# Four-layer hybrid of attention and experts on one core: image 1's chunks of layer 1 taken half by half, with what follows an image spread over steps

## The chip, the core and the metric

The kernel runs on one core of one Trainium2 chip. The metric is the device time of one execution in microseconds (us). The engines are TensorE (PE; its weight loads, PEld, have rows of their own), VectorE (DVE), ScalarE (ACT), GpSimd (POOL) and SyncE (SP), which here only starts DMA transfers. Each engine takes its instructions in the order in which the program lists them; engines wait for each other by semaphores. L12 is line 12 of the kernel before. Matrix products write to PSUM, which has 8 banks of 128 x 512 numbers.

## What is computed

Two images of 256 channels and 32 x 32 places go through four layers; P = 128, N = 1024 places an image, CH = 512, so an image has two halves of 512 columns and eight tokens' tiles of 128. Cut to what matters here:

```python
# layer 0: group norm, attention over both images together
x = x + _L0_conv_ref(_gn(x), ...)
# layer 1: each image by itself
xn = (x - mu) * rsqrt(var + EPS) * gn_w + gn_b          # over a whole image
q, k, v = einsum('oc,bchw->bohw', w_in, xn)             # 8 heads of 64
attn = softmax(einsum('bhdi,bhdj->bhij', q * SCALE, k))
x = einsum('oc,bchw->bohw', w_out, einsum('bhij,bhdj->bhid', attn, v)) + b_out + x
# layer 2: windowed attention, then a mixture: 2 of 8 experts for each token
t = _to_tokens(x)
t = t + _L2_attn_ref(_ln_t(t), ...)
t = t + _L2_ffn_ref(_ln_t(t), ...)
# layer 3: additive attention, then a second mixture
t = t + _L3_attn_ref(_ln_t(t), ...)
t = t + _L3_ffn_ref(_ln_t(t), ...)
```

## The kernel before

**Layers 0 and 1** share one loop over steps, `attention` (L190). Its work is a list of chunks, each a pair of heads against 512 queries, and each chunk has steps over 128 keys: 64 steps in layer 0, 8 in layer 1. A step has a score (L215, L216 on PE, the exponential `e` of L218 on ACT, the running sum L227 on DVE) and an accumulation (L237 on PE). Scores run one step ahead of accumulations, two at a chunk's start. At a chunk's end ACT and DVE copy the accumulated `o` out of PSUM (L243, L244). Its tile `ps_o` exists once, so the next chunk's first accumulation waits for that copy.

Everything else hangs on steps by number: a dictionary `todo` maps a step to functions that are called after it (L268 to L292). Two steps after a chunk's end comes `divide` (L247): a row matmul L251 sums over the partitions, ACT copies the total (L257), DVE adds the two halves of o (L259), takes reciprocals (L263, two halves) and multiplies (L264), and POOL adds the reciprocals to a check (L265). Four steps after the end comes the chunk's `finish`, and four steps before the end the next chunk's `prepare`.

In layer 1 (`front`, L333) an image's norm and values are prepared amid the chunks before it (`norm` L406, `values` L429). `heads` (L438) projects q and k of one pair of heads for a whole image: two halves each, four projections into PSUM banks (L446), copied out by ACT (L450). The chunks go image by image, within it pair by pair, within that half by half (L494); so a pair's `heads` is called in front of its first half, and `finish` does its work only behind an image's last chunk. There it calls `output1` (L452): for two halves and two blocks of channels four matmuls (L457) and an addition to x on DVE (L463). Then `done` (L1427): for each of eight tiles two transposes on PE (L1432), a copy to `t` by DVE or ACT in turn, and then `norms` (L1416): statistics (L144, L145), `normalise` (L147: a square root by 13 small DVE operations, L131 to L138, a shift L153, and eight `u` by ACT, L155), and `to_channels` (L176: transposes L182 into `ps_row` banks, copied out by DVE, L186, and ACT, L184). All of these banks and those of L251, L446 and L457 come from one pool of two, taken in turn.

**Layer 0's projections** (`project0`, L509) run over four blocks of 512 columns. Ahead of blocks 0 and 2 stands the group norm of image 0 and 1 (`group_norm` L576, matmuls L542, `xn` L546), and then a block's keys, queries (L530) and values (L567).

**Behind layer 1** the window attention (L618) takes four groups of 512 tokens; POOL adds a bias to t's tiles (L647, each once its `u` is made), the groups' projections are L684, the scores L711. Then experts: a block of 128 tokens has two parts, each a step of a generator (`experts`, L1070: `turn` L1109, `up` L1126, `middle` L1137, `down` L1148), about one part for each call of `second.step()`. Image 0's blocks are done first; then `prepare` (L1526) combines its experts' results: a tile's two rows `yt` are loaded by SP and ACT queues (L1200), DVE adds them (L1202) and takes statistics; then come norm, projection (L1251) and, in the additive attention (L1266), `th` sums by DVE (L1285) and tangents by ACT (L1295). `prepare` has 12 steps: eight tiles, and two for each of two halves. Before, the experts' generator goes on in the last four of them (L1585) and then at every second group of the additive attention.

The order within these bounds is not quite that of the source: a scheduler places instructions when the program is built, so the streams of each engine are read from the built program.

Of the kernel before, what the change touches and what calls it, by code (L numbers as in the profile page):

```python
# [24 lines left out]
F32 = mybir.dt.float32  # L25
# [3 lines left out]
AF = mybir.ActivationFunctionType  # L29
ALU = mybir.AluOpType  # L30
# [57 lines left out]
class Stack:  # L88
# [101 lines left out]
    def attention(self, chunks, pools):  # L190
# [91 lines left out]

        chunks[0]["prepare"]()
        scored = 0
        for n in range(at + 5):
            ahead = 2 if 0 < n < at and steps[n][1] == 0 else 1
            while scored < min(n + ahead + 1, at):
                score(scored)
                scored += 1
            if n < at:  # L290
                accumulate(n)
            for f in todo.pop(n, []):  # L292
                f()
        nc.vector.tensor_reduce(self.extremes[:, 1:2], inverses, AX.X, ALU.max)

    def attention_pools(self, ctx):
# [36 lines left out]
    def front(self, xT, weights, tokens, done):  # L333
# [6 lines left out]
        with ExitStack() as ctx:  # L340
# [94 lines left out]
                    )  # L435
                nc.scalar.copy(v[b][:, i, :], ps)

            def heads(b, pair):  # L438

                for part, to, scale in ((0, q, 0.125), (1, k, 1.0)):  # L440
                    to[b, pair] = two.tile([P, N], F32, name="qh" if part == 0 else "kh")
                    for t in range(N // CH):
                        ps = bank()
                        for c in range(CC):
                            at = part * HID + pair * P
                            nc.tensor.matmul(  # L446
                                ps, lhsT=w_in[:, c, at : at + P], rhs=xn[b][:, c, t * CH : (t + 1) * CH],
                                start=(c == 0), stop=(c == CC - 1),
                            )
                        nc.scalar.activation(to[b, pair][:, t * CH : (t + 1) * CH], ps, AF.Copy, scale=scale)  # L450

            def output1(b):  # L452
                for t in range(N // CH):
                    for o in range(CC):
                        ps = bank()
                        for c in range(PAIRS):
                            nc.tensor.matmul(  # L457
                                ps, lhsT=w_out[:, c, o * P : (o + 1) * P],
                                rhs=oT[b][:, c, t * CH : (t + 1) * CH],
                                start=(c == 0), stop=(c == PAIRS - 1),  # L460
                            )
                        x = xT[:, o, b * N + t * CH : b * N + (t + 1) * CH]
                        nc.vector.scalar_tensor_tensor(x, ps, b_out[:, o : o + 1], x, ALU.add, ALU.add)  # L463

            def chunk1(b, pair, t):
                def prepare():
                    if t == 0 and pair:
                        heads(b, pair)

                def finish():  # L470
                    if pair == PAIRS - 1 and t == N // CH - 1:
                        output1(b)
                        done(b, bank)

                def goes_to():
                    if b not in oT:
                        oT[b] = pools1[1].tile([P, PAIRS, N], F32, name="oT")
                    return oT[b][:, pair, cols]

                cols = slice(t * CH, (t + 1) * CH)  # L480
                return {
                    "prepare": prepare,
                    "n": N // P,
                    "q": lambda: q[b, pair][:, cols],
                    "k": lambda j: [
                        k[b, pair][64 * r : 64 * r + 64, j * P : (j + 1) * P] for r in range(2)
                    ],
                    "v": lambda j: [v[b][:, j, (2 * pair + r) * 64 : (2 * pair + r + 1) * 64] for r in range(2)],
                    "o": goes_to,
                    "finish": finish,  # L490
                }

            chunks = [chunk0(t, o) for t in range(NCH) for o in range(CC)]
            chunks += [chunk1(b, p, t) for b in range(B) for p in range(PAIRS) for t in range(N // CH)]  # L494


            for b, at, first_step, apart in ((0, NCH, 8, 4), (1, NCH * CC + 5, N // P - 2, 1)):
                ready = [lambda b=b: norm(b), *(lambda b=b, i=i: values(b, i) for i in range(N // P))]
                ready += [lambda: None, lambda b=b: heads(b, 0)]
                for i, f in enumerate(ready):  # L500
                    step = first_step + apart * i
                    for c in chunks[at:]:
                        if step < c["n"]:
                            c.setdefault("extras", {}).setdefault(step, []).append(f)
                            break
                        step -= c["n"]
            self.attention(chunks, pools)

    def project0(self, pool, psum, xT, weights, to):  # L509
# [25 lines left out]

        for t in range(NCH):
            cols = slice(t * CH, (t + 1) * CH)
            if t % 2 == 0:
                b = t * CH // N
                mean, rs = self.group_norm(  # L540
                    pool, psum, xT, b,
                    lambda ps, rows: nc.tensor.matmul(ps, lhsT=group, rhs=rows, start=True, stop=True),  # L542
                )
                for at in range(b * N, (b + 1) * N, CH):
                    for c in range(CC):
                        nc.vector.tensor_scalar(  # L546
                            xn[:, c, at : at + CH], xT[:, c, at : at + CH],
                            mean[:, c : c + 1], rs[:, c : c + 1], ALU.subtract, ALU.mult,
                        )


            for o in range(CC):
                ps = project(wk, o, t)
                for r in range(2):
                    mine, other = (slice(64 * a, 64 * a + 64) for a in (r, 1 - r))
                    to = k[mine, 2 * o + r, cols]
                    if r:
                        nc.scalar.activation(to, ps[mine], AF.Identity, bias=bk[mine, o : o + 1])
                    else:
                        nc.vector.tensor_scalar(to, ps[mine], bk[mine, o : o + 1], None, ALU.add)  # L560
                    nc.sync.dma_start(out=k[other, 2 * o + r, cols], in_=to)
# [820 lines left out]
    def run(self):  # L1382
        tc, nc, ins = self.tc, self.nc, self.ins
        PER = N // P
        with ExitStack() as ctx:
            window = ExitStack()
            xw = window.enter_context(tc.tile_pool(name="wa_in", bufs=1, side="right"))
            with tc.tile_pool(name="xT", bufs=1, side="right") as xp:
# [19 lines left out]
                def norm(which, g, bank):  # L1408

                    tiles = slice(4 * g, 4 * g + 4)  # L1410
                    t, u, uT, mv = (have[n] for n in ("t", "u", "uT", "mv"))
                    rs = self.normalise(u[:, tiles], t[:, tiles], mv[:, which, tiles], 1e-5)
                    self.to_channels(uT[:, :, g * CH : (g + 1) * CH], u[:, tiles], bank)
                    return mv[:, which, tiles, 1], rs

                def norms(which, b, bank):  # L1416

# [6 lines left out]
                        self.to_channels(uT[:, :, g * CH : (g + 1) * CH], u[:, 4 * g : 4 * g + 4], bank)  # L1424
                    return mv[:, which, tiles, 1], rs

                def done(b, bank):  # L1427

                    for i in range(b * PER, (b + 1) * PER):
                        ps = bank(0)[:, 0:C].rearrange("p (c d) -> p c d", c=CC)  # L1430
                        for c in range(CC):
                            nc.tensor.transpose(ps[:, c, :], xT[:, c, i * P : (i + 1) * P], self.ident)  # L1432
                        to = have["t"][:, i, :].rearrange("p (c d) -> p c d", c=CC)
                        if i % 2:
                            nc.scalar.copy(to, ps)
                        else:
                            nc.vector.tensor_copy(to, ps)
                    norms(0, b, bank)

                self.front(xT, weights, tokens, done)  # L1440
                t, u, uT = (have[n] for n in ("t", "u", "uT"))
# [123 lines left out]
            with ExitStack() as side:  # L1565
# [16 lines left out]
                        inv.close()  # L1582
                    second.step()
                for k, _ in enumerate(prepare(0, bank, enter(side, "outputs2"), PER, nc.sync, nc.scalar)):
                    if k >= PER:  # L1585
                        second.step()


# [43 lines left out]
class General(Stack):  # L1632
# [4 lines left out]
    def front(self, xT, weights, tokens, done):  # L1637
# [2 lines left out]
        self.layer1(xT, *weights())  # L1640
        tokens()
        with self.tc.tile_pool(name="tok_ps", bufs=4, space=PSUM) as psum:
            for b in range(B):
                done(b, lambda k: psum.tile([P, CH], F32, name="tr"))

    def attention(self, chunks, pools):

# [540 lines left out]
```

## Time and profile before

| | |
|---|---|
| time, median of 3 runs | 2505.05 us (2500.96 to 2509.13) |
| profiled execution: its own time | 2506.88 us |
| its span, first to last instruction | 2504.9 us |
| PE, DVE, ACT busy | 94%, 68%, 57% of the span |
| mean clock granted to PE | 0.978 |
| layer 0's first score, layer 1's last row matmul | at 63.5 and 1352.5 us |
| first scores of the window attention | at 1386.1 us |
| image 0's first `yt` starts, first tangent | at 1713.3 and 1746.7 us |

A row of a timeline has the start, the duration, the engine, the line, the operation, what it writes and reads, how many instructions are put together, and in brackets how long the engine had been idle and what released it. A row of waits has who waited, for whom, the total in us, how often, and the longest. A row of busy times by stretch has the length, then the busy us of PE, PEld, DVE, ACT and POOL with their instructions, the clock granted to PE (1 is full), the DMA's share and GB/s.

### The profile page before, as it was taken

The page shows a single profiled execution, that of the slowest core. Times are in us where ns is not written, and L with a number is a line of the kernel's source. Part 1 is how long each engine was busy: PE and PEld are TensorE (multiplying, and loading weights), DVE is VectorE, ACT ScalarE, POOL GpSimd, SP SyncE. Part 2 cuts the span into 40 slices and gives each one's busy share as a digit, 9 for nine tenths or more (in the row PEclk, how much of TensorE's full clock was granted, in tenths as well). Part 3 has the DMA queues.
Part 4 walks back from the last instruction along what each step waited for, and adds up shares of the span by engine and source line. Part 5 has one row for each costly group of instructions (what it writes and reads, how often), then busy time and mean ns, then how long its engine had stood idle before and what let it go on. Part 6 is the DMA issues. An engine that isn't in the chain of part 4 may idle for free.

```text
span 2504.9 us, 42385 instructions
## 1 busy us (share of the span) xinstructions
PE 2350.2 (94%) x17211; PEld 1024.5 (41%) x17211; DVE 1701.1 (68%) x2616; ACT 1436.9 (57%) x1626; POOL 241.6 (10%) x254
## 2 busy tenths in 40 slices
PE   7999999999999999999999969997999988889997
PEld 4333333333333333333333536664444432334664
DVE  5677777775677777876578566326877788886543
ACT  1565556545555566544454333222999999999222
POOL 0000000000000000000001312221110000111342
PEclk9999999999999999999999989998999999999998
DMA  4000000000000000000000036775343202122896
GB/s 139 1 1 1 1 1 1 1 1 1 1 1 1 1 2 1 1 1 1 1 2 9 3 117 244 297 289 208 137 141 136 90 14 78 66 91 93 305 323 236
DMA packets 58928, 190.50 MB, mean 76 GB/s; under 512 B 14116, under 2 KB 28964, under 8 KB 48740
## 3 DMA queue, kind: packets, MB, share of 16 engines
q1 hardware_dynamic: 45236, 161.86, 18.3%
q0 software_dynamic: 8160, 22.29, 2.5%
q10 hardware_dynamic: 5328, 3.55, 0.5%
q8 instruction: 137, 2.24, 0.4%
q14 instruction: 67, 0.55, 0.1%
HBM read 168.15 MB, written 17.43 MB: 74 GB/s over the span
## 4 chain that ended last, share of the span: by engine, by line
PE 70%; DVE 11%; issue 7%; ACT 6%; DMA 3%; POOL 1%; SPq 0%; ACTq 0%; DVEq 0%; POOLq 0%
PE ps_o L237 20%; PE ps_t L215 19%; PE ps_e L1304 7%; PE bk_h L1130 4%; PE bk_y L1154 4%; ACT th L1295 3%; DVE sum L227 2%; PE ps_row L446 2%; PE ps_pt L1325 2%; DVE th L1285 2%; PE ps_qk L530 1%; PE ps_row L432 1%; DVE den L263 1%; DMA w<-in_l_w 1%; PE ps_row L457 1%
## 5 line engine op out<-in xcount | busy, mean ns | idle before, releaser
L227 DVE TENSOR_TENSOR sum<-sum,e 128x1024 f32<-128x1024 f32 x592 | 724.9, 1224 | 303.5 <-ACT e L218 292.6
L218 ACT ACTIVATE e<-ps_t 128x1024 f32<-128x1024 f32 x640 | 653.4, 1025 | 464.9 <-PE ps_t L216 463.4
L237 PE MATMUL ps_o<-e,v 64*64 64x512 f32 x5120 | 677.0, 592 | 8.5 <-DVE o L244 7.9
L215 PE MATMUL ps_t<-q,k 64*64 64x512 f32 x2048 | 533.0, 591 | 0.5 <-DVE v L571 0.5
L216 PE MATMUL ps_t<-q,k 64*64 64x512 f32 x2048 | 533.0, 591 | 0.0
L1285 DVE TENSOR_SCALAR th<-kT,qb 128x1024 f32<-128x1024 f32 x478 | 331.2, 749 | 90.2 <-PE ps_e L1304 87.9
L237 PEld LDWEIGHTS ps_o<-e,v 64*64 64x64 f32 x5120 | 194.1, 132 | 370.8 <-issue 179.4
L1295 ACT ACTIVATE th<-th 128x4096 f32<-128x4096 f32 x94 | 335.8, 3651 | 5.2 <-DVE th L1285 5.2
L1146 ACT ACTIVATE h<-bk_t,w 128x128 f32<-128x128 f32 x496 | 142.5, 375 | 267.2 <-issue 149.8
L1304 PE MATMUL ps_e<-th,pick 128*32 128x512 f32 x2048 | 270.2, 621 | 25.4 <-ACT p L1357 15.0
L215 PEld LDWEIGHTS ps_t<-q,k 64*64 64x64 f32 x2048 | 149.2, 133 | 287.2 <-issue 152.9
L1130 PE MATMUL bk_h<-w,xgT 128*128 128x512 f32 x496 | 242.9, 606 | 10.3 <-DVE xgT L1118 9.9
L1154 PE MATMUL bk_y<-w,h 128*128 128x256 f32 x992 | 247.9, 385 | 3.0 <-issue 1.0
L1154 PEld LDWEIGHTS bk_y<-w,h 128*128 128x128 f32 x992 | 178.3, 192 | 48.7 <-issue 24.0
L1135 DVE COPY hp<-bk_h 128x512 f32<-128x512 f32 x124 | 85.3, 688 | 121.6 <-PE bk_h L1130 121.5
L265 POOL TENSOR_TENSOR inverses<-inverses,den 128x512 f32<-128x512 f32 x24 | 30.5, 1269 | 1325.0 <-DVE den L263 1325.0
L216 PEld LDWEIGHTS ps_t<-q,k 64*64 64x64 f32 x2048 | 149.3, 133 | 0.0
L215 PE MATMUL ps_t<-qh,kh 64*64 64x512 f32 x512 | 139.4, 602 | 0.0
L216 PE MATMUL ps_t<-qh,kh 64*64 64x512 f32 x512 | 138.5, 600 | 0.0
L1304 PEld LDWEIGHTS ps_e<-th,pick 128*32 128x32 f32 x2048 | 58.3, 112 | 172.0 <-issue 115.2
L1161 POOL DMA_INDIRECT given<-y,gives x85 | 87.0, 1023 | 428.8 <-DVE y L1160 358.4
L1130 PEld LDWEIGHTS bk_h<-w,xgT 128*128 128x128 f32 x496 | 86.9, 193 | 80.8 <-issue 54.8
(335 smaller groups left out, 2053.6 us busy)
## 6 DMA issues: line engine op xcount, KB each, us to landing
w<-in_l_w SPq DMA_DIRECT2D x39, 1152.0 KB, 5.4
w<-in_l_w SPq DMA_DIRECT2D x39, 1030.0 KB, 7.0
w<-in_l_w SPq DMA_DIRECT2D x46, 640.0 KB, 6.7
w<-in_l_w SPq DMA_DIRECT2D x46, 514.0 KB, 5.4
rows<-u SPq DMA_DIRECT2D x8, 512.0 KB, 3.7
yt<-given SPq DMA_DIRECT2D x24, 128.0 KB, 2.3
k<-k SPq DMA_DIRECT2D x16, 128.0 KB, 2.2
uT<-given ACTq DMA_DIRECT2D x16, 128.0 KB, 4.1
```

The lines of the kernel that those rows point to most:

```text
L215: nc.tensor.matmul(ps[part, 0, :], lhsT=ka[:, part], rhs=q[0:64, :], start=True, stop=True)
L216: nc.tensor.matmul(ps[part, 1, :], lhsT=kb[:, part], rhs=q[64:128, :], start=True, stop=True)
L218: nc.scalar.activation(e, ps, AF.Exp)
L227: nc.vector.tensor_tensor(c["sum"], c["sum"], e, ALU.add)
L237: nc.tensor.matmul(c["po"][64 * r : 64 * r + 64, half, :], lhsT=v[part, :], rhs=e[part, r, :], start=(j == 0), stop=(j == c["n"] - 1),)
L1130: nc.tensor.matmul(ps, lhsT=inputs[b][:, c, :], rhs=first[b][:, at : at + CH], start=(c == 0), stop=(c == CC - 1),)
L1146: nc.scalar.activation(hidden[b, n][:, cols], ps[:, cols], AF.Gelu, bias=first[b][:, at : at + 1])
L1154: nc.tensor.matmul(sums[b], lhsT=h[:, j * P : (j + 1) * P], rhs=second[b][:, at : at + C], start=(n == 0 and j == 0), stop=(n == HH - 1 an ...
L1161: nc.gpsimd.indirect_dma_start(out=given[b], out_offset=index(slots(b)[1], b), in_=y, in_offset=None)
L1285: nc.vector.tensor_scalar(h[:, j, :], *keys_and_queries(n, j), None, ALU.add)
L1295: nc.scalar.activation(h, h, AF.Tanh)
L1304: nc.tensor.matmul(scored[i][U * j : U * (j + 1), a, :], lhsT=aa["pick"][:, m, :], rhs=h[:, j, a * CH : (a + 1) * CH], start=(m == 0), sto ...
```

## The change

Four edits; what is computed stays the same.

1. Image 1's chunks go half by half: all four pairs of its first half, then all four of the second. `heads` now projects k (both halves) with a pair's first half, and q of one half at a time. Image 0 keeps its order. The keys of pairs 2 and 3 of image 1 are put into the place of image 0's values, since they are now held over both halves.
2. What follows an image is a list of small functions, one for each of the next steps: for each half two outputs, four tiles (`token`, now with its statistics) and one norm over four tiles. Image 0's fourteen come after its last chunk, image 1's seven of the first half after its chunk of pair 3, first half, and seven of the second half at the end.
3. In `project0` the group norm of image 1 stands ahead of block 1 instead of block 2.
4. In image 0's combination one more `second.step()` is called, after the third tile.

```diff
-        for n in range(at + 5):
+        n = 0
+        while n < at or todo:
...
             for f in todo.pop(n, []):
-                f()
+                for i, g in enumerate(f() or []):
+                    later(n + 1 + i, g)
+            n += 1
...
-            def heads(b, pair):
-                for part, to, scale in ((0, q, 0.125), (1, k, 1.0)):
-                    to[b, pair] = two.tile([P, N], F32, name="qh" if part == 0 else "kh")
-                    for t in range(N // CH):
...
+            def heads(b, pair, t):
+                for i in (t,) if b else range(0 if t else N // CH):
+                    q[b, pair, i] = two.tile([P, CH], F32, name="qh", bufs=4)
+                    project(b, pair, 0, i, q[b, pair, i])
+                if t:
+                    return
+                if b and pair >= 2:
+                    if not spare:
+                        spare.append(pools1[0].tile([P, N // P, HID], F32, name="v"))
+                    at = (pair - 2) * (N // CH)
+                    k[b, pair] = spare[0][:, at : at + N // CH, :].rearrange("p a d -> p (a d)")
+                else:
+                    k[b, pair] = two.tile([P, N], F32, name="kh")
+                for i in range(N // CH):
+                    project(b, pair, 1, i, k[b, pair][:, i * CH : (i + 1) * CH])
...
                 def prepare():
-                    if t == 0 and pair:
-                        heads(b, pair)
+                    if pair or t:
+                        heads(b, pair, t)
 
                 def finish():
-                    if pair == PAIRS - 1 and t == N // CH - 1:
-                        output1(b)
-                        done(b, bank)
+                    if pair == PAIRS - 1 and (b or t):
+                        follow = []
+                        for i in (t,) if b else (0, 1):
+                            follow += [lambda i=i, o=o: output1(b, i, o) for o in range(CC)]
+                            follow += done(b * (N // CH) + i, bank)
+                        return follow
...
-            chunks += [chunk1(b, p, t) for b in range(B) for p in range(PAIRS) for t in range(N // CH)]
+            chunks += [chunk1(0, p, t) for p in range(PAIRS) for t in range(N // CH)]
+            chunks += [chunk1(1, p, t) for t in range(N // CH) for p in range(PAIRS)]
...
-            if t % 2 == 0:
-                b = t * CH // N
+            if t < B:
+                b = t
...
-                    rs = self.normalise(u[:, tiles], t[:, tiles], mv[:, which, tiles], 1e-5)
+                    self.normalise(u[:, tiles], t[:, tiles], mv[:, which, tiles], 1e-5, scalar=which == 0)
...
-                def done(b, bank):
-                    for i in range(b * PER, (b + 1) * PER):
...
-                    norms(0, b, bank)
+                def token(i, bank):
...
+                    stats(0, i)
+                def done(g, bank):
+                    return [*(lambda i=i: token(i, bank) for i in range(4 * g, 4 * g + 4)), lambda: norm(0, g, bank)]
...
-                    if k >= PER:
+                    if k == 2 or k >= PER:
                         second.step()
```

In the built programs PE has 17214 rows of instructions before and after, ACT, POOL and SP keep their numbers too, and DVE has more, since a square root's 14 small operations are now made for four tiles at a time and not for eight.

More of the change, by code (lines that the diff above doesn't have):

```diff
@@ L436, in values @@
                 nc.scalar.copy(v[b][:, i, :], ps)
-            def heads(b, pair):
-                for part, to, scale in ((0, q, 0.125), (1, k, 1.0)):
-                    to[b, pair] = two.tile([P, N], F32, name="qh" if part == 0 else "kh")
-                    for t in range(N // CH):
[L443 to L463, printed above, removed]
+            def project(b, pair, part, t, to):
+                ps = bank()
+                for c in range(CC):
+                    at = part * HID + pair * P
+                    nc.tensor.matmul(
+                        ps, lhsT=w_in[:, c, at : at + P], rhs=xn[b][:, c, t * CH : (t + 1) * CH],
+                        start=(c == 0), stop=(c == CC - 1),
+                    )
+                nc.scalar.activation(to, ps, AF.Copy, scale=1.0 if part else 0.125)
@@ new lines, in front @@
+            spare = []
+            def heads(b, pair, t):
[13 more added lines that the diff above has]
+                    project(b, pair, 1, i, k[b, pair][:, i * CH : (i + 1) * CH])
@@ new lines, in output1 @@
+            def output1(b, t, o):
+                ps = bank()
+                for c in range(PAIRS):
+                    nc.tensor.matmul(
+                        ps, lhsT=w_out[:, c, o * P : (o + 1) * P], rhs=oT[b][:, c, t * CH : (t + 1) * CH],
+                        start=(c == 0), stop=(c == PAIRS - 1),
+                    )
+                x = xT[:, o, b * N + t * CH : b * N + (t + 1) * CH]
+                nc.vector.scalar_tensor_tensor(x, ps, b_out[:, o : o + 1], x, ALU.add, ALU.add)
@@ L483, in chunk1 @@
                     "n": N // P,
-                    "q": lambda: q[b, pair][:, cols],
+                    "q": lambda: q[b, pair, t],
                     "k": lambda j: [
@@ L493, in front @@
             chunks = [chunk0(t, o) for t in range(NCH) for o in range(CC)]
-            chunks += [chunk1(b, p, t) for b in range(B) for p in range(PAIRS) for t in range(N // CH)]
+            chunks += [chunk1(0, p, t) for p in range(PAIRS) for t in range(N // CH)]
+            chunks += [chunk1(1, p, t) for t in range(N // CH) for p in range(PAIRS)]
             for b, at, first_step, apart in ((0, NCH, 8, 4), (1, NCH * CC + 5, N // P - 2, 1)):
                 ready = [lambda b=b: norm(b), *(lambda b=b, i=i: values(b, i) for i in range(N // P))]
-                ready += [lambda: None, lambda b=b: heads(b, 0)]
+                ready += [lambda: None, lambda b=b: heads(b, 0, 0)]
                 for i, f in enumerate(ready):
@@ L1411, in norm @@
                     t, u, uT, mv = (have[n] for n in ("t", "u", "uT", "mv"))
-                    rs = self.normalise(u[:, tiles], t[:, tiles], mv[:, which, tiles], 1e-5)
+                    self.normalise(u[:, tiles], t[:, tiles], mv[:, which, tiles], 1e-5, scalar=which == 0)
                     self.to_channels(uT[:, :, g * CH : (g + 1) * CH], u[:, tiles], bank)
-                    return mv[:, which, tiles, 1], rs
                 def norms(which, b, bank):
@@ L1425, in norms @@
                     return mv[:, which, tiles, 1], rs
-                def done(b, bank):
-                    for i in range(b * PER, (b + 1) * PER):
[L1430 to L1437, printed above, removed]
-                    norms(0, b, bank)
+                def token(i, bank):
+                    ps = bank(0)[:, 0:C].rearrange("p (c d) -> p c d", c=CC)
+                    for c in range(CC):
+                        nc.tensor.transpose(ps[:, c, :], xT[:, c, i * P : (i + 1) * P], self.ident)
+                    to = have["t"][:, i, :].rearrange("p (c d) -> p c d", c=CC)
+                    if i % 2:
+                        nc.scalar.copy(to, ps)
+                    else:
+                        nc.vector.tensor_copy(to, ps)
+                    stats(0, i)
+                def done(g, bank):
+                    return [*(lambda i=i: token(i, bank) for i in range(4 * g, 4 * g + 4)), lambda: norm(0, g, bank)]
                 self.front(xT, weights, tokens, done)
@@ L1642, in front @@
         with self.tc.tile_pool(name="tok_ps", bufs=4, space=PSUM) as psum:
-            for b in range(B):
-                done(b, lambda k: psum.tile([P, CH], F32, name="tr"))
+            for g in range(NCH):
+                for f in done(g, lambda k: psum.tile([P, CH], F32, name="tr")):
+                    f()
     def attention(self, chunks, pools):
```

## The prediction

> **What bounds the kernel now.** I read the page's busy times and the chain that ended last first, then TensorE's (PE's) own list of waits, then the timelines around the places that the diff touches.
>
> ```profile
> PE 2350.2 (94%) x17211; PEld 1024.5 (41%) x17211; DVE 1701.1 (68%) x2616; ACT 1436.9 (57%) x1626; POOL 241.6 (10%) x254
> ...
> PE 70%; DVE 11%; issue 7%; ACT 6%; DMA 3%; POOL 1%; SPq 0%; ACTq 0%; DVEq 0%; POOLq 0%
> ```
>
> PE is busy for 94% of the span and carries 70% of the chain. PE's instructions are the same in both built programs (17214 in each); only their order differs. So the change can move the time by nothing but PE's waits and by the clock that PE gets. All waits of PE for a release that the changed places own are in these rows (line, what it waited for: total us, times, longest us):
>
> ```profile
> PE bk_t L1141 <- ACT h L1146: 9.9, 3, 7.2
> ...
> PE ps_o L237 <- DVE o L244: 7.9, 7, 1.2
> PE ps_gs L542 <- DVE gn_mv L586: 7.5, 1, 7.5
> PE ps_qk L530 <- DVE xn L546: 6.6, 2, 3.4
> ...
> PE ps_row L182 <- ACT u L155: 5.9, 5, 3.0
> ```
>
> The reader is to see how small they are: everything that spreading image 0's and image 1's follow-up can win is L182's 5.9 us and part of L237's 7.9, plus what the clock loses after a wait. That loss shows at image 0's norm:
>
> ```profile
> 1207.77 0.59 PE L237 MATMUL ps_o<-e,v 64*64 64x512 f32 x1
> 1210.73 0.33 PE L182 MATMUL ps_row<-ident,u 128*128 128x128 f32 x1 [2.38 <-ACT u L155]
> ```
>
> ```profile
> 1210.00:1219.00 9.00, 8.11 (x23) 2.71 (x23) 1.63 (x4) 6.13 (x11) 0.00 (x0) 0.62 0.01 2
> ```
>
> PE stands 2.4 us, and then (busy times of that stretch, the clock behind POOL's column) gets a clock of 0.62 for 9 us, which is 3.4 us of work lost. The price of that wait is 2.5 + 3.4 = 5.9 us.
>
> What VectorE (DVE) does in one chunk of image 1 decides the rest:
>
> ```profile
> 1247.34 1.23 DVE L227 TENSOR_TENSOR sum<-sum,e 128x1024 f32<-128x1024 f32 x1 [0.79 <-ACT e L218]
> 1248.92 3.36 DVE L263 RECIPROCAL den<-total 128x256 f32<-128x256 f32 x2 [0.36 <-ACT total L257]
> 1252.21 1.77 DVE L264 TENSOR_TENSOR oT<-o,den 128x256 f32<-128x256 f32 x2
> 1253.90 5.20 DVE L227 TENSOR_TENSOR sum<-sum,e 128x1024 f32<-128x1024 f32 x4
> 1259.02 0.69 DVE L244 COPY o<-ps_o 128x512 f32<-128x512 f32 x1
> ```
>
> Each chunk's divide holds DVE for 3.36 + 1.77 = 5.1 us; then it catches up at 1.23 us for a sum against PE's 1.72 us a step (starts of neighbouring score steps, 1303.32 and 1305.04). It runs late for half a chunk, and whatever stands behind the reciprocals in its queue is late with it.
>
> **The follow-up, spread (image 0 both halves, image 1's first half).** Before, an image's eight tokens were normed after the last divide had long gone by. Now there are three sets of two outputs, four tokens and a norm, each amid the next chunks. I followed each set along the built program's queues, with R for the start of the divide's row matmul L251. DVE starts the reciprocals at R + 1.9 (1224.88 to 1226.79). Norm chain: 13 small operations at 0.2 us (1206.37 to 1210.05, one sum of 1.2 taken off) and a shift; statistics 0.36; the first u 0.5 and 0.15 to reach PE.
>
> Set 1 (image 0, tokens 0 to 3): DVE's queue holds reciprocals, last token's statistics, sum, 7 small operations, sum, 6 more, shift: 1.9 + 3.4 + 0.4 + 1.2 + 0.1 + 1.4 + 1.2 + 1.2 + 0.2 + 0.65 = R + 11.65. PE comes to the norm's transposes after the row (1.0), the last token (0.43), two steps (3.44) and a quarter of a third (1.07): R + 5.95. **Wait 5.7 us.** Behind it on PE stand the rest of that accumulation, the next scores, three projections and two outputs; ScalarE (ACT) has the four u's ahead of the next exponential, and DVE waits for that exponential, so nobody else gets ahead.
>
> Set 2 (image 0, tokens 4 to 7): the chain stands ahead of the reciprocals. From the last token's transposes PE has one step, the row and half a score: 3.15. DVE needs 0.1 + 0.4 + two statistics 0.9 + 2.4 + sum 1.2 + 0.4 + 0.65 = 6.1. **Wait 3.0.** Then the first transposed bank is emptied only behind reciprocals and products (5.1), and the next projection wants that bank: PE is there at about 11.0, the bank free at 12.9. **Wait 1.9.**
>
> Set 3 (image 1, first half): reciprocals and products both ahead, with two sums and the chain behind: 1.9 + 3.4 + 1.8 + 0.4 + 1.2 + 0.7 + 1.2 + 2.0 + 0.2 + 0.65 = R + 13.4; PE is there at R + 6.2. **Wait 7.2.**
>
> Together 17.8. After each, the clock and the pacing by ACT's u's (0.5 us each): the nearest rows are 3.4 (above) and 1.5 (0.96 over 38 us from 1352, where a wait of 3.0 lies). I take 2.8 a set, 8.4. Sum **+26.2**; bounds: +13 (half the waits, 1.5 each) and +34 (POOL's add of L265, 1.26 us, also holds each set's sum up; 3.4 for each clock, and 2 more for waits as long as these).
>
> [...]
>
> **What goes.** Image 0's wait above: -5.9. L237's waits for o in image 1: three of 1.2 us (the rows of that stretch say 3.6, 3 times), each at the end of a chunk that has no projections in it; now every chunk but the last has 1.7 us of projection (7.13 us for four, L446), which is more than 1.2: -3.6 (bounds 0 and -3.6).
>
> **The end of image 1.** Before, from the last row matmul PE lost 1.3 at tokens, 3.3 for u and 1.6 by the clock. Now half of the outputs and tokens are gone from there (PE does them earlier, at the same price), and with them cover. The last two outputs' first three products (5.1) end 0.9 before oT (6.0 after the row; a bias product, L641, fills half). Then tokens and eight projections of the window stage hold PE for 9, while DVE needs 12: POOL's adds L647 now start ahead of the chain, and beside those adds small DVE operations took 0.65 to 0.71 instead of 0.17 (1374.02 to 1379.5). 0.5 + 3.0 + 1.6 + 1.0 against 6.2: I take 0, bounds -4.7 (chain not held up) and +3.
>
> **First group norm.** Moved from ahead of t = 2 to ahead of t = 1. Before:
>
> ```profile
> 36.75 0.35 PE L542 MATMUL ps_gs<-gs_d,group 128*128 128x2 f32 x2 [1.15 <-DVE gs_d L606]
> 40.48 5.28 PE L530 MATMUL ps_qk<-xn,sb_wk 128*128 128x512 f32 x8 [3.37 <-DVE xn L546]
> ```
>
> 1.15 + 3.37 and 1.7 by the clock (5.28 for what takes 3.6 elsewhere): 6.2. Now xn is long ready at t = 2, but PE's first average stands behind statistics that DVE starts only behind t = 0's v: 25.55 + 3.0 = 28.5 against PE's 25.2, so 3.4, then 1.1, then the same 1.7: 6.2. Net **0**, bounds -1.7 and +1.7. Image 1's data were there at 25.55 without a wait, and SP's k copies keep their place.
>
> **The experts' part amid image 0's combination.**
>
> ```profile
> 1711.92 1.89 PE L1154 MATMUL bk_y<-w,h 128*128 128x256 f32 x8
> 1721.03 1.12 PE L1141 MATMUL bk_t<-ident,hp 128*128 128x128 f32 x4 [7.22 <-ACT h L1146]
> 1726.77 2.08 PE L1130 MATMUL bk_h<-w,xgT 128*128 128x512 f32 x2 [4.62 <-DVE xgT L1118]
> ```
>
> PE has 11.8 us idle here, and a part is 4.2 us of PE (8.33 us a block, two parts). But the end of the stage is set by DVE: combinations, norm, u at 1729.4, keys, first tangent at 1746.7. The part puts y, hp and three half xgT into that queue ahead of u (0.4 + 0.7 + 1.1), and the last xgT waits for PE to have finished the part: u at about 1733.8, **+4.4**. ACT takes four gelus between its DMA issues, so the last yt goes out at 1720.2 instead of 1720.05. SP's fetches and POOL's scatter of the part come that much earlier and are waited for by nobody there. In the stage after it, where ACT is busy 49.9 of 50 us and PE 48.8, the part's 4.2 us of PE (or only ACT's 1.1) are gone: -2.4. Net **+2**, bounds -4 and +4.4.
>
> **Sum** against the profiled execution (2506.9; span 2504.9 and 2.0 around it): 26.2 - 5.9 - 3.6 + 0 + 0 + 2 = +18.7, so 2525.6. The median of the three runs, 2505.05, is 1.8 lower: **2524**. A measurement of this kernel tells about 0.3%, 7.5 us, from no change.
>
> **Rivals.**
> Faster: the norm's chain is done when PE comes to the transposes at L182. A set then costs nothing there, and what goes wins: -5.9 - 3.6 and about -2 at the ends: 2505 - 11 = 2494. The sign turns where the three sets cost 11.5 together, 3.8 each. For: set 2's chain stands ahead of the reciprocals, and a PE that is 5 us later than I count would meet it everywhere. Against: the reciprocals' 3.36 us lie in each of 24 chunks, and nothing in sets 1 and 3 lets the chain pass them. 0.13.
> Nothing to be seen: the sets cost some 13, the lower bound: 2505 + 13 - 9.5 = 2508. For: the waits may overlap with a clock that is low anyway. 0.17.
> Much slower: the clock stays half through the transposes that ACT's u's pace, as after the 7.2 and 4.6 above (0.80 over 35 us from 1710, 7 us lost); then each set costs 4 more: 2537. 0.15.
> My forecast, 2512 to 2532: 0.55. So faster 0.13, same 0.17, slower 0.70. The range leaves out most of the faster case and takes in the others: 2500 to 2538.
>
> **What would show it.** Right: between 1200 and 1330 three waits of L182 for u of about 6, 3 and 7 us, each with a clock below 1 behind it; a projection L446 that waits for uT's copy; in image 1 no wait for o but perhaps one; u of the combination some 4 us later with a shorter wait for h; the start of the first scores as before, near 63.5. Wrong: L182's waits in sum as before, or layer 1 ending earlier than at 1386 (the window scores' start, now expected near 1402).

## The result, and the profile after

The change makes the kernel slower: 2532.41 us in the median of four runs (2529.9 to 2535.3) against 2505.89 in four runs of before taken beside them, a ratio of 1.0107 (95% interval 1.0093 to 1.0121). The profiled execution took 2535.32 us with a span of 2533.0, so it is some 3 us longer than the median.

Lines of the kernel after are shifted: L446, L450 and every line up to L284 have the same numbers as before; L475 are the output products (L457 before), L1451 the tokens' transposes (L1432), L564 and L552 the first group norm and its projections (L542, L530), L706 and L762 the window's projections and averages (L684, L740), L1163 and L1152 the experts' (L1141, L1130). The page of after, busy times and the chain by engine:

```profile
PE 2370.5 (94%) x17211; PEld 1030.1 (41%) x17211; DVE 1705.3 (67%) x2644; ACT 1435.6 (57%) x1626; POOL 241.9 (10%) x254
...
PE 71%; DVE 11%; issue 7%; ACT 6%; DMA 3%; POOL 1%; SPq 0%; ACTq 0%; DVEq 0%; POOLq 0%
```

PE has the same 17211 matmul records and 20.3 us more busy time: much of the loss is not idle time but work at a lower clock, which takes 51.2 us of PE's busy time in after and 35.5 in before (busy time times what the granted clock was below 1; its mean is 0.971 for 0.978). PE's waits over the whole kernel after, in the rows that the prediction showed of before:

```profile
PE ps_row L182 <- ACT u L155: 18.3, 4, 6.1
...
PE ps_gs L564 <- DVE gn_mv L608: 11.0, 2, 7.5
...
PE bk_t L1163 <- ACT h L1168: 5.3, 3, 2.8
...
PE ps_o L237 <- DVE o L244: 4.2, 4, 1.2
...
PE ps_qk L552 <- DVE xn L568: 3.3, 1, 3.3
```

L182 went from 5.9 to 18.3 us, L237's waits for o from 7.9 to 4.2. The waits of the group norm only changed rows (7.5 + 6.6 before, 11.0 + 3.3 after). PE's timeline shows L182's four waits, those of the sets 1, 2 and 3 and of the last set, at the end of image 1:

```profile
1221.02 1.39 PE L182 MATMUL ps_row<-ident,u 128*128 128x128 f32 x4 [5.46 <-ACT u L155]
...
1255.94 0.33 PE L182 MATMUL ps_row<-ident,u 128*128 128x128 f32 x1 [2.27 <-ACT u L155]
...
1335.37 0.69 PE L182 MATMUL ps_row<-ident,u 128*128 128x128 f32 x2 [6.11 <-ACT u L155]
...
1402.88 0.69 PE L182 MATMUL ps_row<-ident,u 128*128 128x128 f32 x2 [4.41 <-ACT u L155]
```

What holds set 1 up stands in DVE's timeline:

```profile
1210.73 3.37 DVE L263 RECIPROCAL den<-total 128x256 f32<-128x256 f32 x2 [0.35 <-ACT total L257]
1214.02 0.37 DVE L144 BATCH_NORM_STATS2 ln_st<-t 128x6 f32<-128x256 f32 x1
1214.30 2.29 DVE L227 TENSOR_TENSOR sum<-sum,e 128x1024 f32<-128x1024 f32 x1
...
1217.87 1.22 DVE L227 TENSOR_TENSOR sum<-sum,e 128x1024 f32<-128x1024 f32 x1
...
1220.17 0.16 DVE L153 SCALAR_TENSOR_TENSOR nm_shift<-mv,rs 128x4 f32<-128x4 f32 x1
```

The reciprocals stand ahead of the last statistics, the sums between them and the small operations, and the shift ends 11.5 us after the start of the row matmul (1208.82); PE had come to the transposes at 1215.56.

Where the time is, stage by stage in the profiled executions (lengths in us; each stage ends at the event named, the last at the end of PE's last instruction and the others at a start):

| stage, until | before | after | e3 | e9 | e12 |
|---|---|---|---|---|---|
| first score | 63.5 | 65.0 | 65.5 | 65.1 | 64.7 |
| window's first average (L740, L762) | 1327.0 | 1346.6 | 1346.9 | 1322.8 | 1324.4 |
| first expert's transpose | 104.7 | 105.7 | 106.5 | 103.9 | 104.4 |
| image 0's first `yt` start | 218.1 | 222.5 | 217.5 | 215.3 | 216.8 |
| first tangent | 33.5 | 36.2 | 34.5 | 34.8 | 36.2 |
| last tangent | 558.2 | 557.9 | 560.6 | 558.3 | 556.8 |
| PE's last instruction | 191.5 | 190.5 | 191.4 | 190.9 | 188.7 |

19.6 of the 28 us lie in the second row, and there in layer 1 and what follows it: layer 0, from its first score to layer 1's, takes 929.7 us for 929.6. The 4.4 us in the experts' blocks and the 1.5 at the start cannot be told from scatter: over all 14 profiles of this study the blocks took 212.2 to 222.5 us and the first score came at 62.9 to 65.8, whichever edits a kernel had.

### The profile page after: what moved, and what is told of

The parts are those of the page before. It is cut to its first block, busy times and chain, and to the rows that moved or that the text cites. A ratio compares the mean times of both kernels' runs of the same rounds, so it can differ in the third digit from the quotient of the medians.

```text
span 2533.0 us, 42411 instructions
## 1 busy us (share of the span) xinstructions
PE 2370.5 (94%) x17211; PEld 1030.1 (41%) x17211; DVE 1705.3 (67%) x2644; ACT 1435.6 (57%) x1626; POOL 241.9 (10%) x254
## 4 chain that ended last, share of the span: by engine, by line
PE 71%; DVE 11%; issue 7%; ACT 6%; DMA 3%; POOL 1%; SPq 0%; ACTq 0%; DVEq 0%; POOLq 0%
PE ps_o L237 20%; PE ps_t L215 20%; PE ps_e L1326 6%; PE bk_y L1176 4%; PE bk_h L1152 4%; ACT th L1317 3%; PE ps_row L446 2%; DVE sum L227 2%; DVE th L1307 2%; PE ps_pt L1347 2%; PE ps_qk L552 1%; PE ps_row L436 1%; PE ps_row L475 1%; PE bk_t L1163 1%; DVE den L263 1%
## 5 line engine op out<-in xcount | busy, mean ns | idle before, releaser
L237 PE MATMUL ps_o<-e,v 64*64 64x512 f32 x5120 | 679.2, 592 | 4.9 <-DVE o L244 4.2
L237 PEld LDWEIGHTS ps_o<-e,v 64*64 64x64 f32 x5120 | 194.1, 132 | 365.2 <-issue 180.0
L1152 PE MATMUL bk_h<-w,xgT 128*128 128x512 f32 x496 | 244.4, 608 | 10.8 <-DVE xgT L1140 10.0
L1152 PEld LDWEIGHTS bk_h<-w,xgT 128*128 128x128 f32 x496 | 87.5, 193 | 78.1 <-issue 54.2
L1123 POOL DMA_INDIRECT xg<-rows,takes x85 | 89.3, 1050 | 276.3 <-PE bk_x L1135 223.3
L215 PE MATMUL ps_t<-qh,kh 64*64 64x512 f32 x384 | 105.0, 603 | 0.0
```

The source lines that it names most:

```text
L215: nc.tensor.matmul(ps[part, 0, :], lhsT=ka[:, part], rhs=q[0:64, :], start=True, stop=True)
L237: nc.tensor.matmul(c["po"][64 * r : 64 * r + 64, half, :], lhsT=v[part, :], rhs=e[part, r, :], start=(j == 0), stop=(j == c["n"] - 1),)
L1123: nc.gpsimd.indirect_dma_start(out=tokens[b], out_offset=None, in_=rows(b)[:, :], in_offset=index(slots(b)[0], b))
L1152: nc.tensor.matmul(ps, lhsT=inputs[b][:, c, :], rhs=first[b][:, at : at + CH], start=(c == 0), stop=(c == CC - 1),)
```

## The experiments

My theory: readers of a norm's result stand in in-order queues for a chain that DVE finishes some 5 us too late, and the clock adds to it. Rivals: the other edits; the order half by half in itself; follow-up work strewn among steps in itself; DVE as the bound. Each time stands beside runs of before on the same chip (medians 2508.92 for e1 to e4, 2505.23 for e5 to e8, 2508.51 for e9 to e11, 2506.11 for e12). The ratios are the recorded ones and not the quotients of these medians; the quotient is 1.0076 for e3, 1.0051 for e4, 1.0090 for e8 and 1.0122 for e10, and within 0.0006 of the ratio elsewhere.

| | kernel | time, us | ratio (95% interval) |
|---|---|---|---|
| e1 | before + first group norm moved | 2509.03 | 0.9998 (0.9985 to 1.0012) |
| e2 | before + experts' part | 2508.91 | 1.0000 (0.9984 to 1.0016) |
| e3 | follow-up and order alone | 2527.89 | 1.0056 (1.0037 to 1.0076) |
| e4 | e3 with image 1 in the old order | 2521.72 | 1.0043 (1.0029 to 1.0057) |
| e5 | e3, u and transposes later | 2513.47 | 1.0036 (1.0019 to 1.0054) |
| e6 | e3, transposes alone later | 2516.20 | one run |
| e7 | e3, whole norm later | 2513.34 | one run |
| e8 | e3, waits filled with matmuls | 2527.77 | 1.0079 (1.0063 to 1.0096) |
| e9 | e3, u on POOL, transposes later | 2503.48 | 0.9981 (0.9964 to 0.9998) |
| e10 | e8 with half the filling | 2539.07 | 1.0136 (1.0110 to 1.0162) |
| e11 | order alone, follow-up in bursts | 2518.52 | 1.0045 (1.0031 to 1.0058) |
| e12 | the whole change, u on POOL | 2506.29 | 1.0004 (0.9990 to 1.0018) |

**e1 and e2: the two small edits.** In before:

```diff
-            if t % 2 == 0:
-                b = t * CH // N
+            if t < B:
+                b = t
```

> The kernel before with only the first group norm of image 1 moved from ahead of t = 2 to ahead of t = 1. My theory: its waits change place and not size (3.4 + 1.1 us at the averages ahead of t = 1 for 1.15 + 3.37 us at t = 2, and 1.7 us by the clock on both sides), so the first score starts within 1.5 us of the 63.48 us of before and the time within 2 us of 2505.9. Rival: the first queries and keys of t = 1 stay at a low clock behind the new wait, and the 1.5 us by which the first score of the changed kernel is late (65.02) are all this edit's; then 2507.4. Either way it is no part of the 27 us that matters.

First score at 63.3 us; e3, without this edit, has it at 65.5. So the edit is worth nothing that these runs can show, and the 1.5 us of the changed kernel are not its.

```diff
-                    if k >= PER:
+                    if k == 2 or k >= PER:
                         second.step()
```

> The kernel before with only the experts' part amid image 0's combination. My theory: first tanh about 3 to 4 us later against the first yt copy than before, some 2 us of it won back in the additive stage; total +1.5 to +2, 2507 to 2508, and the blocks between 1495 and 1713 as long as before (218.1 us). Rival: the 4.4 us by which the blocks of the changed kernel took longer (222.5 for 218.1) come from this edit, by the fetches that it moves on SP's queue; then the blocks are 222 us long here too, and the time is about 2512.

The blocks took 216.6 us, and the time is not the 2512 of the rival that blamed SP's queue, so that rival falls. From the first `yt` to the first tangent it took 36.8 us instead of 33.5, and nothing of that came back (558.2 us of tangents before, 561.5 here).

**e3 and e4: follow-up and order.** e3 is the change without those two edits. e4 is e3 with

```diff
-            chunks += [chunk1(1, p, t) for t in range(N // CH) for p in range(PAIRS)]
+            chunks += [chunk1(1, p, t) for p in range(PAIRS) for t in range(N // CH)]
...
-                    if pair == PAIRS - 1 and (b or t):
+                    if pair == PAIRS - 1 and t:
...
-                        for i in (t,) if b else (0, 1):
+                        for i in (0, 1):
```

> The changed kernel without the moved group norm and without the experts' part amid the combination: image 1 half by half and the spread follow-up alone. My theory: nearly all of the loss is here. Three waits at L182 for u of 5.5, 2.3 and 6.1 us, a clock near 0.5 to 0.6 behind each, a wait of 4.4 us at the last norm; +18 to +23 up to the window stage's end, 2524 to 2530. Rival: the loss is shared by the late stages, and this kernel stands at 2518 or below.

> As the kernel with the follow-up alone, but image 1 in the old order (pair by pair, both halves) with its whole follow-up behind the last chunk: only image 0's follow-up is spread. My theory: two sets are left (waits 5.5 and 2.3 us, 4.4 and 1.4 us by the clock, 13.5 in all), image 0's old wait goes (-5.9) and the waits for o in image 1 go by the projections that now stand ahead of each chunk (-2 to -3.6): +4 to +6, 2510 to 2512. Rival: the half-by-half order itself costs nothing but its third set, or the spread alone costs the whole loss: then 2520 or above. Second rival: spreading image 0's follow-up wins and only the order loses: below 2505.

e3 has the waits of the changed kernel to 0.02 us (5.47, 2.27, 6.12, 4.41), and layer 1 takes 1346.9 us. e4 was meant to lose 4 to 6 us and lost 11 by its ratio (7 to 14): its two sets wait as foreseen (5.47 and 2.27), but a third cost that I had not seen joins them at the end of image 1. There the follow-up goes half by half now, and on PE the second half's outputs stand behind the first half's norm. The waits from 1180 to 1410:

```profile
PE ps_row L182 <- ACT u L155: 13.2, 3, 5.5
PE ps_row L251 <- DVE sum L227: 2.7, 1, 2.7
PE ps_mm L706 <- ACT qh L711: 1.1, 1, 1.1
PE ps_row L1451 <- DVE xT L480: 0.7, 1, 0.7
```

13.2 less 5.47 and 2.27 leaves 5.4 us at the first half's norm, for the 3.0 of before.

**e5, e6, e7: readers later.** In e5 a set's functions, one to a step and in shorthand, are

```diff
-  [*tokens, norm]
+  [*tokens, chain, nothing, nothing, nothing, scaled, nothing, turned]
```

with `chain` DVE's square root and shift, `scaled` ACT's four u, `turned` PE's transposes. e6 calls `scaled` with `chain`, e7 the whole norm after the three empty steps.

> The kernel with the follow-up alone, but of each norm only DVE's chain (1/sqrt and shift) stays in its step; ACT's four u come four steps later and PE's transposes of them two steps after those. DVE's queue is the same. My theory (who reads the chain's result comes 5 us too early): the waits at L182 of 5.5, 2.3 and 6.1 us go, and the low clock behind them (6.7 to 8.3 us in all three) with them; against the follow-up alone -20 to -22, so 2506 to 2509 beside 2508.9 for before; the wait at the last norm (4.4 us) stays. First rival (what costs is that follow-up work is strewn among the steps: switches between small transposes and scores, PE's banks, ACT's extra work): the waits go but the time falls by less than half of that, to 2518 or more. Second rival: the waits return in another row (scores for exponentials, projections for banks), and the time hardly falls.

> As above, but ACT's four u stay with the chain and only PE's transposes come four steps later. My theory: ACT then stands in its queue for the chain (some 5 us for sets 1 and 3, 2 for set 2) with the next exponentials behind it, so L182 waits no more but PE stands at L237 for e, or at L215 for a score bank, for what is left after PE's lead of one to two steps (1.7 to 3.4 us): 2 to 4 us each for sets 1 and 3. Span between the two. Rival: only PE's own place matters, ACT has slack for it (busy 57%): then no wait is left and the span is that of the kernel where both come later.

> The follow-up alone, but each norm as a whole (chain, u and transposes) three steps later, so that the divide's reciprocals are done with when DVE comes to the chain. My theory: sets 1 and 3 lose what the reciprocals hold the chain up by and keep the chain's own length, as set 2 has it now: three waits of 2 to 3.5 us in place of 5.5, 2.3 and 6.1, each with a low clock behind it; 6 to 9 us of the wait and clock go. Rival (the chain itself with its sums between is what takes the time, not the reciprocals): waits of 5 us or more stay.

I had expected e5 to come out as before; it stands 8 us above. In none of the three does L182 wait amid the steps any more, and in each, waits of 4 to 5.5 us stand elsewhere. e5's waits of PE from 1180 to 1420, ACT's timeline and PE's around set 1:

```profile
PE ps_o L237 <- ACT e L218: 7.8, 3, 5.1
PE ps_row L182 <- ACT u L1472: 4.4, 1, 4.4
PE ps_row L446 <- ACT qh L450: 4.0, 1, 4.0
```

```profile
1211.56 1.02 ACT L218 ACTIVATE e<-ps_t 128x1024 f32<-128x1024 f32 x1 [0.75 <-PE ps_t L216]
1218.82 0.60 ACT L1472 ACTIVATE u<-t,nm_shift,rs 128x256 f32<-128x256 f32 x1 [6.23 <-DVE nm_shift L1468]
1219.32 0.58 ACT L450 ACTIVATE qh<-ps_row 128x512 f32<-128x512 f32 x1
```

```profile
1214.47 1.45 PE L446 MATMUL ps_row<-xn,sb_l_w_in 128*128 128x512 f32 x3
1219.95 2.08 PE L446 MATMUL ps_row<-xn,sb_l_w_in 128*128 128x512 f32 x2 [4.03 <-ACT qh L450]
```

ACT stands 6.23 us at the first u with the copy of a projection behind it, and PE then waits for that copy. The shift ends 11.53 us after the row matmul in all three kernels (sets 1; 12.2 in sets 3), as in the changed one. The edits did not do to ACT and DVE what I had written: in sets 1 and 3 the scheduler put chain and u where they had been, u two exponentials behind the last token's copy, and only PE's transposes moved. So e7 says nothing of reciprocals and chain apart, and the three runs are one experiment: freeing PE alone takes away about half, since ACT still stands in line. From layer 1's first score to the window's first average e3 is 19.8 us longer than before; in e5 8.7 of these are left, in e6 12.3 and in e7 10.5.

**e8 and e10: is it the clock?** Ahead of the transposes:

```diff
+                    if which == 0:
+                        ps = bank(0)
+                        for _ in range((12, 5, 14, 10)[g]):
+                            nc.tensor.matmul(ps, lhsT=self.ident, rhs=xT[:, 0, 0:CH], start=True, stop=True)
```

> The follow-up alone, with 12, 5, 14 and 10 matmuls of 128x512 (0.43 us each) that nobody reads ahead of the transposes of the four norms; PE works through its waits. The output is the reference's. It takes nothing from the waits: u comes when it came. What it tells is the price of the clock: by the profile 3 to 4.4, 1.7 to 3.3, 2 and 4 us behind the four waits. My theory: L182's waits shrink to under 1 us each, the granted clock stays 1.0 through the sets, and the time falls by 11 to 14 against the follow-up alone, to 2514 to 2517. Rival: the clock behind a wait costs nothing, since the transposes are paced by ACT's u there anyway; then the time stays at 2526 to 2530.

> The kernel with filled waits again, with half the filling (6, 2, 7 and 5 matmuls; one was meant as 0.43 us and takes 0.87, so the first filling lasted 35.8 us for 18.3 us of waits). Now 5.2, 1.7, 6.1 and 4.4 us. My theory: PE works through its waits and no longer; the clock stays 1.0 behind all four; 12 us of low clock go and no more than 1 to 2 us are added: -10 to -12 against the follow-up alone, 1.002 to 1.004 of before against its 1.0056 to 1.0079. Rival: a low clock behind the waits costs little, since the u pace the transposes: 1.006 or more again.

A matmul of that shape stands in the records as two of 0.43 us, so e8's filling lasted 35.8 us for 18.3 us of waits. The clock did stay 1.0 behind all four, and from image 1's values to the first window average what PE lost by the low clock fell against e3 from 14.1 to 1.7 us and its idle time from 24.3 to 7.2; but the filling cost as much as that gave. e10 (6, 2, 7, 5) was to be clean and is the slowest of all: the scheduler put the filling two steps earlier than the wait began, so that those steps came behind it, and the exponentials they feed as well.

```profile
1212.22 5.42 PE L1438 MATMUL ps_row<-xT,ident 128*128 128x512 f32 x12
1220.16 1.39 PE L182 MATMUL ps_row<-ident,u 128*128 128x128 f32 x4 [2.53 <-ACT u L155]
```

Both runs fail as a price of the clock; that comes from the traces (last section).

**e11: the order alone.** As e3, but `finish` calls outputs, tokens and norm at once, image 0's eight tokens with one chain.

> Image 1 half by half (with the projections spread over its chunks), but every follow-up at once where its last divide is, as before: image 0's after its last chunk, image 1's first half amid the second half's first chunk, the second half's at the end. My theory: image 0's old wait stays (2.4 us and 3.4 by the clock), the two halves of image 1 have a burst each with a wait of 3 to 5 us and 2 to 4 by the clock, and the waits for o go (-3.6): +3 to +8, 1.001 to 1.003 of before; so most of the 19 to 27 us come from spreading and not from the order. Rival: the order itself is the loss, 1.005 or more.

+10 us by the medians and +11 by the ratio, above the range I gave. Image 0's wait is the old one (2.40, and 0.77 for a bank), the first half's burst waits 3.14 and the last norm 4.40 instead of 3.00; 10.2 us are lost by the low clock there, 5.0 before. So order and spread each cost by themselves: in the table's second row 9.2 us (e11) and 13.3 (e4), and 19.9 together (e3).

**e9: nobody waits for the chain but POOL.** As e6, where `scaled` comes with `chain`, with

```diff
+                            if g < 3:
+                                nc.gpsimd.tensor_scalar(
+                                    u[:, 4 * g + i, :], t[:, 4 * g + i, :],
+                                    mv[:, 0, 4 * g + i, 0:1], got["rs"][:, i : i + 1], ALU.subtract, ALU.mult
+                                )
+                                continue
```

in `scaled`, and `turned` seven steps behind `chain` instead of four.

> The follow-up alone, with the twelve u of the three sets amid the steps computed by POOL instead of ACT, and PE's transposes of them seven steps later; the last set's u stay on ACT. Two runs with later readers left waits of 4 to 5 us where PE waits for a projection's copy or an exponential: in both programs ACT's u stand behind the same two exponentials as without the delay, so ACT waits for DVE's chain there and all its later work waits with it. My theory (who stands in a queue for the chain costs, be it PE or ACT): with nobody but POOL waiting, the waits at L446 and L237 for ACT (11.6 us in the run where u and transposes came later) and the low clock behind the first and third (4 us) go; beside that run -12 to -15, so 2498 to 2502 in that job's terms, 0.996 to 0.999 of before. Rival: DVE itself is the bound there (reciprocals, products, sums and chain, late by itself by 5 us); then the exponentials wait for DVE's sums (four e buffers), waits of 2 to 5 us stay, and the time is 1.002 of before or more.

This is the run that decides. All of PE's waits of 0.3 us or more from 1180 to 1400, and POOL's u of set 1:

```profile
PE ps_row L182 <- ACT u L1478: 4.3, 1, 4.3
PE ps_row L251 <- DVE sum L227: 2.7, 1, 2.7
PE ps_o L237 <- DVE o L244: 1.7, 2, 1.4
PE ps_o L237 <- ACT e L218: 0.3, 1, 0.3
```

```profile
1220.46 6.18 POOL L1473 TENSOR_SCALAR u<-t,mv,rs 128x256 f32<-128x256 f32 x4 [4.90 <-DVE nm_shift L1468]
```

DVE is as late as ever (the shift ends 11.51 us after the row matmul), POOL takes 6.18 us for what took ACT 2.08, and PE waits for none of it: the waits of the three sets are gone and none like them has come in their place. So DVE is not the bound, and strewing work among the steps costs little by itself. e9 differs from e6 in two things, the engine that makes u and three more steps for the transposes. What was left of e6's waits stood behind ACT, so it is the first that answers them; the two were not run apart. The table's second row is 24.1 us shorter than in e3 and 4.2 shorter than before, and the kernel is the only one to beat before, by 0.2%, with an interval that ends just under 1.

**e12: the whole change so.** The same `done` in the changed kernel.

> The changed kernel whole, with the moved group norm and the experts' part, and with the twelve u of the three sets on POOL and their transposes seven steps later. My theory: the loss of the change is the wait of ACT and PE for the norms' chain and the clock behind it, and the other two edits are worth nothing to 2 us: 0.997 to 1.000 of before, and no wait for u but the last one (4.3 us). Rival: group norm and experts' part cost something together with the spread follow-up (the changed kernel measured 1.0107 [1.0093, 1.0121], the follow-up alone 1.0056 [1.0037, 1.0076], each of the two others alone 1.000): then it stands 3 to 5 thousandths above the 0.998 of the follow-up with POOL's u, at 1.001 to 1.003.

From 1180 to 1400 the same waits as in e9, and 1.0004, between my range (to 1.000) and the rival's (from 1.001): the change is repaired down to before, not below it. Whether the two small edits cost something in company stays open: alone they are 1.000 each, but after stands at 1.0107 for e3's 1.0056 (1.0076 by the medians), and e12 at 1.0004 for e9's 0.9981, the last two with overlapping intervals.

## Why the prediction was right, and where not

The direction and the mechanism were right; the time came 8 us above my 2524, at the upper edge of the forecast (2512 to 2532) and within the range. That it came so near is in part luck: the sets cost 4.3 us less than my sum and the end of image 1 4.3 more, and the two errors cancel. By its steps:

- **Three sets**, +26.2 in my sum. Waits 5.46, 2.27 and 6.11 for my 5.7, 3.0 and 7.2; the 1.9 us at a bank that waits for uT did not appear (no such row). The clock behind them took 4.4, 1.7 and 1.9 us (busy time times what the clock was below 1) for my 8.4. In all 21.9. That it comes from queues that stand for DVE's late chain is shown by e9 and e12; that the reciprocals in particular do is read from DVE's rows and was not tested, since e7 did not move the chain.
- **What goes**, -5.9 and -3.6: right. L237's waits fell by 3.7, and the old burst is gone.
- **The end of image 1, "I take 0"**: this term failed. It had the bounds -4.7 and +3 and measured +4.3. The last u came 1.4 us later against PE (4.40 for 3.00), 1.05 us of another wait went, and the clock behind it stood at 0.50 for 10.24 us instead of 3.41 (3.97 us lost for 1.63). The wait for the sum at the last row matmul is 2.7 us in both kernels and cost 1.7 us of clock after it in the new one and nothing in the old. I had read that row as harmless and priced only waits that grew.
- These make 21.9 - 5.9 - 3.7 + 4.3 = 16.6 of the 19.6 us in layer 1. 1.2 more is a longer wait for image 1's xn (1.78 us; e12 has 0.56 with the same four edits). Ahead of image 1's values before lost 1.7 us in 3.4 us at clock 0.50 from 1115.5 on that after does not have. So some 3.5 us remain, and they are neither wait nor clock: from layer 1's first score to the window's first average PE is busy for 389.4 us (994.74 to 1411.64) instead of 378.0 (993.10 to 1390.48), and the low clock takes only 7.0 of these 11.4 (13.7 for 6.7). My sum had no term for PE's own work; which matmuls take longer, and why, was not tested.
- **First group norm**, 0: right (e1).
- **The experts' part**, +4.4 and -2.4: u came 4.1 us later against the first `yt`, as worked out, but the first tangent only 2.7 (3.3 in e2). The 2.4 that the stage behind it was to give back did not come: 557.9 us of tangents in the changed kernel and 561.5 in e2, for 558.2. Net +2.4 in the changed kernel's profile for my +2 (+6.6 in e2's), and nothing that e2's time can show.
- **The rivals.** "Nothing to be seen" fell with 1.0107. "Much slower" was close in time (2537), but its mechanism, a clock that stays half because ACT's u pace the transposes, fits set 1 alone of the three (10.2 us at half clock; 6.8 in e3). "Faster" named its condition, that the chain be ready when PE comes, and e9 makes that true by sending PE there later: -5 us instead of the -11 I gave it; the end of image 1, which still costs some 4, would make up most of the difference.

## What to carry to other kernels

When a chain on a busy engine is late, look for every in-order queue that holds a reader of it, not only for the one the trace shows idle: here freeing PE moved the wait to ACT (6.23 us in e5), and a queue with little else to do (POOL, 6.18 us for what took ACT 2.08) took it away. Check in the built program that a delay moved what it was to move. And price a wait by the clock behind it as well as by its length: set 2's 2.27 us had 3.42 us at clock 0.50 behind them in after, 1.7 us lost.

## What the runs showed of the hardware

PE's granted clock is 1.00 or 0.50 wherever the traces of before and after record it. In after it fell, between 1190 and 1405 us, at 1219.67, 1257.21, 1332.31, 1380.09 and 1400.57, and stayed low for 10.24, 3.42, 6.82, 3.42 and 10.24 us. These lengths are 3, 1, 2, 1 and 3 times the shortest, and the falls stand 11, 22, 14 and 6 times that apart, to 0.2 us. The rows below cut the time into neighbouring stretches of 3.41 us, counted from the falls of each trace; the last column but two is the clock. First the wait at the last row matmul in after, then the same wait of 2.7 us in before (columns: length, then the busy us of PE, PEld, DVE, ACT and POOL).

```profile
1376.68:1380.09 3.41, 0.74 (x8) 0.00 (x0) 3.20 (x4) 0.58 (x1) 0.00 (x0) 1.00 0.00 0
1380.09:1383.51 3.42, 3.41 (x6) 1.13 (x7) 2.26 (x5) 0.69 (x2) 0.00 (x0) 0.50 0.00 0
```

```profile
1347.62:1351.04 3.42, 1.89 (x16) 0.21 (x8) 3.21 (x3) 1.61 (x2) 0.00 (x0) 1.00 0.00 0
1351.04:1354.45 3.41, 1.98 (x7) 0.69 (x8) 2.58 (x5) 0.69 (x2) 0.00 (x0) 1.00 0.00 0
1354.45:1357.86 3.41, 3.41 (x9) 1.52 (x8) 3.41 (x3) 0.00 (x0) 0.00 (x0) 1.00 0.00 0
```

In after all of the wait fell into one stretch (0.74 us busy of 3.41), and the next ran at half clock; in before it lay across two (1.53 and 1.43 us idle), and nothing followed. Cut in the same way between 1190 and 1405 us, these two traces have seven full-clock stretches with 2.10 us or more idle, and each was followed by one at half clock; of those with 1.52 us or less idle none was. So the same wait cost 1.7 us more in after and nothing in before, and it lay differently to these stretches; no run moved it alone.
